# Token choice spread over periods 0 to 8, expert work in periods 9 to 14, and one scatter-add for two experts

## The chip, the cores and the metric

The kernel runs on one NeuronCore of a Trainium2 chip. The metric is the device time of one execution in microseconds (us): before the change the median of three runs is 1363.7 us, with 1360.01 and 1367.55 us as the lowest and the highest. The engines are named as the profile names them: PE (matmuls; PEld is its weight load), DVE (vector), ACT (scalar and activation functions), POOL (GpSimd, which also issues the indirect DMAs) and SP (which issues all other DMAs). Each engine works through its own queue in order. An instruction that waits therefore holds up everything behind it on its engine.

## What is computed

The program computes two layers of a transformer for 32 sequences of 256 tokens, 8192 tokens of width 128, all in fp32. The change touches only the first layer's mixture of experts (MoE):

```python
xn = layernorm(x)
s  = attn0(xn)                                   # two attention + MLP blocks
# MoE: 64 experts of width 96, each token chooses 8, each expert holds at most 64 tokens
probs = softmax(xn @ router_w.T);  w, ids = top_k(probs, 8);  w = w / w.sum()
valid = (place of the token in its expert's queue, in token order) < 64
y[e]  = (silu(xb[e] @ w_gate[e]) * (xb[e] @ w_up[e])) @ w_down[e]
moe   = sum over a token's valid experts of w * y   +   shared expert(xn)
x = x + s * silu(moe)
```

A second layer follows (linear attention and a MoE with one expert of 32 for each token). It starts from the sums of the first layer, and the change leaves it as it is.

## The kernel before

**Periods.** The 8192 tokens are 16 groups of 512. Two groups make a pair `p`, and a pair passes through the two attention blocks `l`, so there are 16 units `(p, l)`. The loop `for k in range(units + 2)` works in periods: period `k` does the softmax attention of unit `k`, and beside it (`beside(k)`) the second norm and the widening matmuls of unit `k-1`, the narrowing matmuls of unit `k-2`, and the norm and the projections of unit `k+1`. These are generators that `run` takes in turn, a step of each at a time. They set the order in which the program is written. The Tile framework then schedules the instructions onto the engines' queues when the program is built, and that order is fixed at run time.

**The token choice** is more generators in the same periods. `enter(g)` loads and norms a group and writes it to a table in device memory (`tab0`). `choose(p)` takes router logits, exponentials and the eight largest of 64 for each token (L400 and L401 on DVE), writes the weights to `tab0` (L411) and makes a key row for each expert (L418). `shared(g)` is the shared expert (L427 to L439). `search(k)` finds, for a quarter of the tokens, each expert's 64 first tokens: eight rounds of MAX8 and MATCH_REPLACE8 over 1024 keys (L446 and L447). After the last quarter `places()` merges the four quarters (L457 to L474) and leaves the row numbers `gidx` and `sidx`. Which pairs are chosen in which period stands in the dictionary `choosing`, and the quarters stand in `searched`; `share(k)` takes the pairs chosen in period `k-1`.

**The experts.** `experts(q)` handles four experts. It loads their weights, gathers 2 x 128 rows from `tab0` with two indirect DMAs on POOL (L485; rows 0 to 63 are an even expert's, 64 to 127 an odd one's), transposes them (L492), and runs gate and up (L499) and down (L511). Four ACT copies (L519) scale the result by each token's weight. Four indirect DMAs with an add (L523), each of 64 rows, put it into two tables, `moe0[0]` for even and `moe0[1]` for odd experts, in turn. A scatter-add waits until the one before it on the same table has landed. There are 16 such calls, two in each of periods 7 to 14.

**What follows.** `route(g)` starts the second layer. Its loads of `moe0` (L184 and L186) wait for the last scatter-add, POOL adds the two tables (L187), and ACT takes the activation (L191). The first `route` steps are written beside periods 15 to 17.

**Buffers** that the change meets: an expert's weights, gathered rows and scaled outputs (`e_wg`, `e_wd`, `e_gx`, `e_y`) have two buffers each, and the PSUM banks of tag `mm` are two. At the period where the choice has ended, its tiles are freed (`cf.close()`) and the first tiles of the second layer are laid out in their place. The flag `early` of `softmax` gives half of the probability scalings (L607) to ACT instead of DVE (L609).

Of the kernel before, what the change touches and what calls it, by code (L numbers as in the profile page):

```python
# [16 lines left out]
F32 = mybir.dt.float32  # L17
I32 = mybir.dt.int32
U32 = mybir.dt.uint32
AF = mybir.ActivationFunctionType  # L20
ALU = mybir.AluOpType
# [4 lines left out]
P = 128  # L26
BATCH, SEQ, D = 32, 256, 128
T = BATCH * SEQ
# [5 lines left out]
E0, K0, C0, F0 = 64, 8, 64, 96  # L34
# [26 lines left out]
def recurrent_kernel(ctx: ExitStack, tc: tile.TileContext, x, consts, small0, wsd, wgu, wd, small1, bias1, wr, out):  # L61
    nc = tc.nc
    vec, act, pool, pe, sp = nc.vector, nc.scalar, nc.gpsimd, nc.tensor, nc.sync
# [6 lines left out]
    dram = ctx.enter_context(tc.tile_pool(name="dram", bufs=1, space=DRAM))  # L70
    psum = ctx.enter_context(tc.tile_pool(name="psum", bufs=4, space=PSUM))

    def bank(tag="mm", bufs=2):
        return psum.tile([P, GW], F32, tag=tag, name=f"ps_{tag}", bufs=bufs)

    tab0 = dram.tile([T + P, D + E0], F32, name="tab0")

    moe0 = [dram.tile([T + P, D], F32, name=f"moe0_{i}") for i in range(2)]
    xslot = dram.tile([S1 * P, D + 1], F32, name="xslot")
    back = dram.tile([T + S1 * P, D], F32, name="back")  # L80
    moe1 = dram.tile([T, D], F32, name="moe1")
# [69 lines left out]
    def room(pool_, gs):  # L151
        for g in gs:
            x_at[g] = pool_.tile([P, GT, D], F32, name=f"x_{g}")
            xt_at[g] = pool_.tile([P, GW], F32, name=f"xt_{g}")
            if g % 4 == 0:
                hots[g // 4] = pool_.tile([P, NT // 4, E1], F32, name=f"hot_{g // 4}")
# [132 lines left out]
    def rolling(steps, lag):  # L289

        live, n = [], 0
        while n < len(steps) or live:
            if n < len(steps):
                live.append(steps[n])
                n += 1
            for _ in range(lag):
                for i in list(live):
                    if next(i, live) is live:
                        live.remove(i)
                    yield  # L300

    def begin(g):
        yield from route(g)
        if g >= INL:
            yield from shared1(g)


    with ExitStack() as c0:


        w0 = c0.enter_context(tc.tile_pool(name="w0", bufs=1, side="right"))
        wk = c0.enter_context(tc.tile_pool(name="wk0", bufs=2, side="right"))
# [130 lines left out]
        def largest(dst, src):  # L443
            for r in range(C0 // 8):
                c8 = dst[:, r * 8 : (r + 1) * 8]
                vec.max(c8, src)  # L446
                found.append(vec.match_replace(out=src, in_to_replace=c8, in_values=src, imm_value=0.0))  # L447
                yield

        gidx = w0.tile([P, E0 // 2], I32, name="gidx")  # L450
        sidx = w0.tile([C0, E0], I32, name="sidx")

        def places():
            top = wf.tile([P, C0], F32, name="top", bufs=1)
            yield from largest(top, cand.rearrange("p q c -> p (q c)"))
            both = wf.tile([E0, 2 * C0], F32, name="both", bufs=1)
            vec.tensor_copy(both[:, :C0], top[:E0])  # L457
            ps = bank()
            pe.matmul(ps[:E0, :C0], ident[:, E0:], top, start=True, stop=True)
            vec.tensor_copy(both[:, C0:], ps[:E0, :C0])  # L460
            first = wf.tile([E0, C0], F32, name="first", bufs=1)
            yield from largest(first, both)

            slot = wf.tile([E0, 2, C0], F32, name="slot", bufs=1)
            vec.scalar_tensor_tensor(slot[:, 0], first, 0.0, ciota, ALU.is_equal, ALU.mult)
            vec.tensor_tensor(slot[:, 0], slot[:, 0], first, ALU.subtract)
            vec.tensor_scalar(slot[:, 0], slot[:, 0], float(T), None, ALU.add)
            vec.tensor_copy(slot[:, 1], slot[:, 0])
            ps = bank()
            pe.transpose(ps[:, :E0], slot.rearrange("e h c -> e (h c)"), ident[:E0, :E0])  # L470
            pairs = ps[:, :E0].rearrange("p (j h) -> p j h", h=2)
            vec.tensor_copy(gidx[:C0], pairs[:C0, :, 0])
            vec.tensor_copy(gidx[C0:], pairs[C0:, :, 1])
            vec.tensor_copy(sidx, ps[:C0, :E0])  # L474
            yield

        def experts(q):

            wg = wk.tile([P, 4, 2 * F0], F32, name="e_wg")
            sp.dma_start(wg, wgu[:, 4 * q : 4 * q + 4])  # L480
            wdn = wk.tile([F0, 4, D], F32, name="e_wd")
            sp.dma_start(wdn, wd[:, 4 * q : 4 * q + 4])
            gx = wk.tile([P, 2, D + E0], F32, name="e_gx")
            for h in range(2):
                pool.indirect_dma_start(  # L485
                    out=gx[:, h], out_offset=None, in_=tab0,
                    in_offset=bass.IndirectOffsetOnAxis(ap=gidx[:, 2 * q + h : 2 * q + h + 1], axis=0),
                )
                yield
            pt = bank("tr", 2)  # L490
            for h in range(2):
                pe.transpose(pt[:, h * P : (h + 1) * P], gx[:, h, :D], ident)  # L492
            xg = wk.tile([P, 4 * C0], F32, name="e_xg")
            act.copy(xg, pt[:, : 4 * C0])
            yield
            gu = bank()
            for u in range(2):
                for e in range(4):
                    pe.matmul(  # L499
                        gu[:F0, (4 * u + e) * C0 : (4 * u + e + 1) * C0], wg[:, e, u * F0 : (u + 1) * F0],  # L500
                        xg[:, e * C0 : (e + 1) * C0], start=True, stop=True,
                    )
            hs = wk.tile([F0, 4 * C0], F32, tag="h", name="e_h")
            act.activation(hs, gu[:F0, : 4 * C0], AF.Tanh, scale=0.5)
            vec.scalar_tensor_tensor(hs, hs, 1.0, gu[:F0, : 4 * C0], ALU.add, ALU.mult)
            vec.tensor_tensor(hs, hs, gu[:F0, 4 * C0 :], ALU.mult)
            yield
            yp = bank()
            for e in range(4):
                at = (e % 2) * C0  # L510
                pe.matmul(  # L511
                    yp[at : at + C0, (e // 2) * D : (e // 2 + 1) * D], hs[:, e * C0 : (e + 1) * C0], wdn[:, e],
                    start=True, stop=True,
                )
            yield
            ye = wk.tile([C0, 4, D], F32, tag="y", name="e_y")
            for e in range(4):
                at, col = (e % 2) * C0, D + 4 * q + e
                act.activation(  # L519
                    ye[:, e], yp[at : at + C0, (e // 2) * D : (e // 2 + 1) * D], AF.Copy,  # L520
                    scale=gx[at : at + C0, e // 2, col : col + 1],
                )
                pool.indirect_dma_start(  # L523
                    out=moe0[e % 2], out_offset=bass.IndirectOffsetOnAxis(ap=sidx[:, 4 * q + e : 4 * q + e + 1], axis=0),
                    in_=ye[:, e], in_offset=None, compute_op=ALU.add,
                )
                yield

# [180 lines left out]
        qkv, wide, mid = {}, {}, {}  # L709
# [25 lines left out]


        entered = {0, 1}
        choosing = {0: (0,), 1: (1, 2), 2: (3,), 3: (4, 5), 4: (6,), 5: (7,)}
        searched = {2: (0,), 3: (1,), 4: (2,), 6: (3,)}

        def front(k):

# [21 lines left out]
        def share(k):  # L764
            for p in choosing.get(k - 1, ()):
                for g in (2 * p, 2 * p + 1):
                    yield from shared(g)

        def some(steps, n):
            for _ in zip(range(n), steps):  # L770
                yield

        begun = rolling([begin(g) for g in range(NG)], 2)
        for k in range(units + 2):
            if k == 7:
                cf.close()
                works.append(ctx.enter_context(tc.tile_pool(name="first_work", bufs=1)))
                begin1(ctx.enter_context(tc.tile_pool(name="first", bufs=1)))
            if k == 16:
                ca.close()  # L780
                works.append(ctx.enter_context(tc.tile_pool(name="mid_work", bufs=2)))
                room(ctx.enter_context(tc.tile_pool(name="mid", bufs=1)), range(EARLY, 9))
            steps = [beside(k), front(k), search(k), share(k)]
            steps += [experts(q) for q in range(E0 // 4) if 7 + q // 2 == k]
            if k < units:
                gs, l = unit(k)
                steps = [softmax(gs, l, qkv, k < 7), *steps]
            more = {15: 10, 16: 20, 17: 12}.get(k)
            if more:
                steps.append(some(begun, more))  # L790
            drain(run(*steps))
# [3 lines left out]
    wk = ctx.enter_context(tc.tile_pool(name="wk1", bufs=2))  # L795
# [37 lines left out]
    ps = bank()  # L833
# [285 lines left out]
```

## Time and profile before

| | |
|---|---|
| median of three runs | 1363.7 us (1360.01 to 1367.55) |
| the profiled execution | 1377.67 us, span 1375.7 us |
| PE, DVE, ACT, POOL busy | 90%, 69%, 57%, 50% of the span |
| granted TensorE clock, mean | 0.963 |
| scatter-adds L523 | 64, 92.5 us on POOL, mean 1445 ns |
| gathers L485 | 32, each 1010 ns in a steady period |
| last scatter-add starts at | 730.5 us |

The profiled execution is 14 us longer than the median of the runs, so differences within it are read rather than its total. Matmuls are pipelined and their ends are modelled, so PE "busy" is not PE at its peak. A period is read off from the first of the 16 softmax exponentials (L600) of its unit: period 1 runs from 64.1 to 121.8 us, period 7 from 403.8 to 451.2, period 14 from 710.0 to 766.6.

### The profile page before, as it was taken

To read this page: it belongs to the slowest core of one execution; us is meant where nothing else is said; L and a number is where in the kernel's file an instruction comes from. 1 tells how busy PE (TensorE), PEld (TensorE's weight loads), DVE (VectorE), ACT (ScalarE), POOL (GpSimd) and SP (SyncE) were. 2 spreads that over 40 slices of the span, in tenths; PEclk is the share of its full clock that TensorE was granted. 3 is DMA by queue.
4 is the path that set the end of the run, shared out by engine and by line. 5 is a ranking of instruction groups with operands and counts; after the bars stand their busy time and mean duration, and the time that the engine had idled before them with its cause. 6 is when DMAs were issued, how large, how long until landed. Compare 5 with 4: busy or idle time off the path is not lost.

```text
span 1375.7 us, 22877 instructions
## 1 busy us (share of the span) xinstructions
PE 1239.4 (90%) x7425; PEld 870.5 (63%) x7425; DVE 944.6 (69%) x3079; ACT 777.5 (57%) x1842; POOL 686.8 (50%) x1052
## 2 busy tenths in 40 slices
PE   6988999899989999999997968799988899999797
PEld 4545665656655776667765655566565678788763
DVE  4679898978965566665665865777756565656437
ACT  1775556576646667676674665443634545545343
POOL 6354428272246766667646463533665343443440
PEclk9999999999989999999998988899999999999999
DMA  6021323310221222122201141413110557666567
GB/s 188 11 54 54 105 84 98 102 45 16 93 72 37 55 49 46 21 50 55 49 9 37 47 125 45 121 36 116 34 41 31 164 180 214 198 194 199 180 197 206
DMA packets 135591, 125.81 MB, mean 91 GB/s; under 512 B 17616, under 2 KB 110768, under 8 KB 135344
## 3 DMA queue, kind: packets, MB, share of 16 engines
q1 hardware_dynamic: 123696, 108.57, 26.4%
q0 software_dynamic: 11776, 15.78, 5.0%
q8 instruction: 59, 0.97, 0.3%
q14 instruction: 60, 0.49, 0.1%
HBM read 83.63 MB, written 40.68 MB: 90 GB/s over the span
## 4 chain that ended last, share of the span: by engine, by line
PE 56%; DVE 16%; POOL 9%; ACT 8%; issue 6%; DMA 4%; SPq 0%; POOLq 0%; another core or an unknown queue 0%; ACTq 0%; DVEq 0%
PE ps_mm L680 7%; PE ps_mm L662 6%; PE ps_sc L585 4%; PE ps_mm L626 3%; PE ps_tr L617 3%; PE ps_tr L131 3%; PE ps_mm L557 3%; PE ps_mm L987 2%; PE ps_sc L887 2%; POOL bn_rs L111 2%; PE ps_mm L567 2%; POOL back L992 2%; PE ps_tr L916 2%; PE ps_sc L978 2%; PE ps_mm L640 2%
## 5 line engine op out<-in xcount | busy, mean ns | idle before, releaser
L992 POOL DMA_INDIRECT back<-e_ys,e_toi x96 | 96.3, 1003 | 134.6 <-ACT e_ys L991 113.6
L600 ACT ACTIVATE a_pr<-ps_sc,a_nm 128x256 f32<-128x256 f32 x256 | 119.2, 478 | 68.2 <-DVE a_nm L591 68.1
L110 POOL TENSOR_SCALAR bn_rs<-bn_mv 128x4 f32<-128x4 f32 x112 | 26.2, 234 | 240.9 <-DVE bn_mv L109 216.2
L662 PE MATMUL ps_mm<-xt,sw 128*128 128x512 f32 x256 | 136.5, 638 | 2.6 <-ACT r_ex L397 2.0
L124 POOL TENSOR_SCALAR z<-s_rows,bn_rs 128x128 f32<-128x128 f32 x256 | 128.6, 514 | 6.9
L680 PE MATMUL ps_mm<-sw,m_h 128*128 128x128 f32 x1024 | 128.7, 280 | 2.9 <-ACT a_at L632 1.1
L680 PEld LDWEIGHTS ps_mm<-sw,m_h 128*128 128x128 f32 x1024 | 120.4, 193 | 14.1 <-issue 4.9
L667 DVE SCALAR_TENSOR_TENSOR m_h<-m_h,m_z 128x512 f32<-128x512 f32 x128 | 88.8, 699 | 48.2 <-ACT m_h L666 47.6
L523 POOL DMA_INDIRECT moe<-e_y,sidx x64 | 92.5, 1445 | 57.8 <-ACT e_y L519 41.2
L111 POOL TENSOR_TENSOR bn_rs<-bn_rs,power 128x4 f32<-128x4 f32 x112 | 113.8, 1016 | 1.3
L664 ACT ACTIVATE m_z<-ps_mm,fold 128x512 f32<-128x512 f32 x128 | 86.9, 687 | 39.1 <-PE ps_mm L662 38.8
L591 DVE TENSOR_REDUCE a_nm<-ps_sc 128x2 f32<-128x512 f32 x128 | 83.1, 680 | 34.9 <-PE ps_sc L585 29.9
L978 PE MATMUL ps_sc<-e_xt,e_w 128*128 128x128 f32 x768 | 100.3, 276 | 3.2 <-ACT e_xt L965 2.2
L978 PEld LDWEIGHTS ps_sc<-e_xt,e_w 128*128 128x128 f32 x768 | 93.1, 192 | 9.6 <-issue 6.4
L585 PE MATMUL ps_sc<-a_qk,a_qk 64*128 64x256 f32 x512 | 96.8, 417 | 0.4 <-ACT a_pr L600 0.3
L617 PEld LDWEIGHTS ps_tr<-con,a_pr 128*128 128x128 f32 x512 | 59.4, 145 | 40.6 <-issue 21.2
L617 PE MATMUL ps_tr<-con,a_pr 128*128 128x128 f32 x512 | 76.3, 283 | 9.4 <-ACT a_pt L618 5.9
L666 ACT ACTIVATE m_h<-m_z 128x512 f32<-128x512 f32 x128 | 80.3, 636 | 1.6
L852 POOL DMA_INDIRECT xslot<-s_rows,dest x64 | 68.3, 1068 | 24.1 <-issue 18.5
L626 PE MATMUL ps_mm<-a_pt,a_v 128*64 128x256 f32 x512 | 73.2, 405 | 5.6 <-ACT e_y L519 2.8
L618 ACT COPY a_pt<-ps_tr 128x512 f32<-128x512 f32 x128 | 70.6, 590 | 9.4 <-PE ps_tr L617 7.9
L987 PE MATMUL ps_mm<-e_w,e_hs 128*128 128x128 f32 x384 | 61.7, 288 | 14.3 <-DVE e_hs L984 10.4
(235 smaller groups left out, 2964.6 us busy)
## 6 DMA issues: line engine op xcount, KB each, us to landing
e_w<-in_wr_dram SPq DMA_DIRECT2D x96, 384.0 KB
xslot<-zero SPq DMA_DIRECT2D x4, 1548.0 KB
e_x<-xslot SPq DMA_DIRECT2D x24, 258.0 KB
e_wg<-in_wgu_dram SPq DMA_DIRECT2D x16, 384.0 KB
x_in<-in_x_dram SPq DMA_DIRECT2D x16, 256.0 KB
tab<-s_rows SPq DMA_DIRECT2D x16, 256.0 KB
moe<-s_y SPq DMA_DIRECT2D x16, 256.0 KB
moe<-zero SPq DMA_DIRECT2D x4, 1024.0 KB
```

The lines of the kernel that those rows point to most:

```text
L111: pool.tensor_tensor(rs[:, 0], rs[:, 0], power, ALU.pow)
L124: ins = pool.tensor_scalar(dst[:, j], src[:, j], rs[:, 1, j : j + 1], rs[:, 0, j : j + 1], ALU.add, ALU.mult)
L523: pool.indirect_dma_start(out=moe0[e % 2], out_offset=bass.IndirectOffsetOnAxis(ap=sidx[:, 4 * q + e : 4 * q + e + 1], axis=0), in_=ye[:, ...
L585: pe.matmul(sc[h][:, j * SEQ : (j + 1) * SEQ], qk[0][hd, q0 : q0 + P], qk[1][hd, b * SEQ : (b + 1) * SEQ], start=True, stop=True,)
L600: act.activation(pr[:, n], sc[h][:, j * SEQ : (j + 1) * SEQ], AF.Exp, bias=nm[:, n : n + 1], accum_out=su[:, n : n + 1],)
L617: pe.transpose(pts[:, n * P : (n + 1) * P], pr[:, n, k * P : (k + 1) * P], ident)
L626: pe.matmul(av[h * DPH : (h + 1) * DPH, :SEQ], v[:, 2 * b + k, h * DPH : (h + 1) * DPH], pt[:, k, h], start=k == 0, stop=k == 1,)
L662: pe.matmul(ps, par("w1", l * FF0 + f * P, P), xt, start=True, stop=True)
L680: pe.matmul(ps[:, j * D : (j + 1) * D], hs[f][:, j * P : (j + 1) * P], par("w2", l * FF0 + f * D, D), start=f == 0, stop=f == 3,)
L978: pe.matmul(ps[:, c * P : (c + 1) * P], wt[:, c * P : (c + 1) * P], xt[:, j * P : (j + 1) * P], start=True, stop=True,)
L987: pe.matmul(yp[:, :D], hs[:, c * P : (c + 1) * P], wt[:, 2 * F1 + c * D : 2 * F1 + (c + 1) * D], start=c == 0, stop=c == 1,)
L992: ins = pool.indirect_dma_start(out=back, out_offset=bass.IndirectOffsetOnAxis(ap=toi[:, j : j + 1], axis=0), in_=ys[:, j], in_offset=None,)
```

## The change

Four edits go together.

1. The two sum tables become the two halves of one table `sums0` of 2 x (8192 + 128) rows, and `sidx` holds, in rows 64 to 127, the odd expert's token numbers plus 8320. One scatter-add now writes 128 rows, an even and an odd expert's together: 32 of them instead of 64. The four scaling copies on ACT remain, two ahead of each scatter-add.
2. One pair is chosen in each of periods 0 to 7 (before: eight pairs in periods 0 to 5, two of them in periods 1 and 3), and the four searches stand in periods 2, 4, 6 and 8 (before: 2, 3, 4 and 6).
3. The 16 expert calls start in period 9 and are dealt out as 3, 3, 3, 3, 2, 2 (before: two in each of periods 7 to 14). In a period of three, the first and the third run one after the other in one chain, and the second runs beside them.
4. The choice's tiles are freed at period 9 instead of 7, and `early` holds until then.

```diff
-    moe0 = [dram.tile([T + P, D], F32, name=f"moe0_{i}") for i in range(2)]
+    sums0 = dram.tile([2 * (T + P), D], F32, name="sums0")
+    moe0 = [sums0[i * (T + P) : (i + 1) * (T + P)] for i in range(2)]
...
-        sidx = w0.tile([C0, E0], I32, name="sidx")
+        sidx = w0.tile([P, E0 // 2], I32, name="sidx")
...
-            vec.tensor_copy(sidx, ps[:C0, :E0])
+            vec.tensor_copy(sidx[:C0], pairs[:C0, :, 0])
+            vec.tensor_scalar(sidx[C0:], pairs[C0:, :, 1], float(T + P), None, ALU.add)
...
-            ye = wk.tile([C0, 4, D], F32, tag="y", name="e_y")
-            for e in range(4):
-                at, col = (e % 2) * C0, D + 4 * q + e
-                act.activation(
-                    ye[:, e], yp[at : at + C0, (e // 2) * D : (e // 2 + 1) * D], AF.Copy,
-                    scale=gx[at : at + C0, e // 2, col : col + 1],
-                )
+            ye = wk.tile([P, 2, D], F32, tag="y", name="e_y")
+            for h in range(2):
+                for u in range(2):
+                    at = slice(u * C0, (u + 1) * C0)
+                    col = D + 4 * q + 2 * h + u
+                    act.activation(ye[at, h], yp[at, h * D : (h + 1) * D], AF.Copy, scale=gx[at, h, col : col + 1])
                 pool.indirect_dma_start(
-                    out=moe0[e % 2], out_offset=bass.IndirectOffsetOnAxis(ap=sidx[:, 4 * q + e : 4 * q + e + 1], axis=0),
-                    in_=ye[:, e], in_offset=None, compute_op=ALU.add,
+                    out=sums0, out_offset=bass.IndirectOffsetOnAxis(ap=sidx[:, 2 * q + h : 2 * q + h + 1], axis=0),
+                    in_=ye[:, h], in_offset=None, compute_op=ALU.add,
                 )
...
-        choosing = {0: (0,), 1: (1, 2), 2: (3,), 3: (4, 5), 4: (6,), 5: (7,)}
-        searched = {2: (0,), 3: (1,), 4: (2,), 6: (3,)}
+        choosing = {0: (0,), 1: (1,), 2: (2,), 3: (3,), 4: (4,), 5: (5,), 6: (6,), 7: (7,)}
+        searched = {2: (0,), 4: (1,), 6: (2,), 8: (3,)}
...
+        def chain(*steps):
+            for i in steps:
+                yield from i
+
+        FIRST, working = 9, (3, 3, 3, 3, 2, 2)
...
-            if k == 7:
+            if k == 9:
...
-            steps += [experts(q) for q in range(E0 // 4) if 7 + q // 2 == k]
+
+            qs = range(sum(working[: max(0, k - FIRST)]), sum(working[: max(0, k - FIRST + 1)]))
+            steps += [chain(*(experts(q) for q in qs[i::2])) for i in range(2)]
...
-                steps = [softmax(gs, l, qkv, k < 7), *steps]
+                steps = [softmax(gs, l, qkv, k < 9), *steps]
```

## The prediction

> **What bounds the kernel now.** I read the page's slices first (PE at 8 to 9 tenths nearly everywhere), then busy time by period, then the groups of one steady period, the waits at the two seams, and the chain of work. Busy time by period (stretch, length, then busy us and count of PE, PEld, DVE, ACT, POOL, the granted clock, DMA share, GB/s); the first row is period 1, the last period 14:
>
> ```profile
> 64.10:121.80 57.70, 50.62 (x246) 29.58 (x246) 48.92 (x192) 36.91 (x99) 31.31 (x63) 0.88 0.18 46
> 121.80:180.00 58.20, 53.06 (x307) 34.48 (x306) 51.16 (x151) 36.29 (x93) 23.63 (x48) 1.00 0.27 87
> 180.00:239.00 59.00, 53.13 (x314) 35.62 (x313) 54.33 (x194) 37.53 (x98) 33.01 (x64) 0.97 0.33 99
> 239.00:298.30 59.30, 53.28 (x307) 34.33 (x306) 52.10 (x163) 36.22 (x92) 28.69 (x59) 1.00 0.25 81
> 298.30:349.40 51.10, 47.88 (x285) 31.12 (x283) 41.16 (x108) 34.71 (x90) 13.96 (x29) 1.00 0.06 16
> 349.40:403.80 54.40, 48.21 (x261) 31.52 (x262) 44.66 (x155) 30.79 (x78) 23.76 (x46) 0.91 0.29 93
> 403.80:451.20 47.40, 44.37 (x292) 30.80 (x289) 27.51 (x82) 30.34 (x80) 26.69 (x35) 0.96 0.19 40
> 494.30:537.50 43.20, 42.87 (x287) 29.77 (x285) 27.87 (x81) 29.86 (x79) 28.79 (x41) 1.00 0.21 44
> 710.00:766.60 56.60, 48.14 (x289) 32.43 (x287) 33.54 (x102) 32.58 (x85) 29.93 (x42) 0.91 0.16 33
> ```
>
> Periods 8 to 13 take 43.1 to 43.2 us each, and PE idles 0.3 us in them: PE is the bound there, and nothing that leaves POOL or DVE helps. Periods 1 to 4 run PE and DVE both at about nine tenths and take 58 to 59 us. The change moves work between these two kinds of period. From 64.1 to 710.0 us it is 645.9 us, all that the change reorders but the end of period 14.
>
> One steady period by group (count, busy us, mean ns):
>
> ```profile
> L523 POOL DMA_INDIRECT moe<-e_y,sidx x8 | 11.5, 1437 | 5.3 <-ACT e_y L519 3.5 <-issue 1.8
> L485 POOL DMA_INDIRECT e_gx<-tab,gidx x4 | 4.0, 1010 | 1.2 <-issue 0.6 <-DMA moe<-e_y,sidx 0.3 <-ACT a_at L632 0.3
> L499 PE MATMUL ps_mm<-e_xg,e_wg 128*96 128x64 f32 x32 | 3.3, 247 | 0.0
> L511 PE MATMUL ps_mm<-e_wd,e_h 96*64 96x128 f32 x16 | 1.3, 285 | 0.0
> L492 PE MATMUL ps_tr<-con,e_gx 128*128 128x128 f32 x4 | 0.8, 286 | 0.0
> ```
>
> The scatter-adds are the largest POOL group, but POOL is busy 28.8 of 43.2 us. Two expert calls cost PE 3.3+1.3+0.8 = 5.4 us by rows; the rows of the period sum to 47.6 against 42.87 busy (neighbours overlap), a factor 0.90, so one call is 2.4 us of PE. The seam in period 6 shows as PE's waits, the other in the chain of work (start, us, what):
>
> ```profile
> PE ps_mm L470 <- DVE bn_mv L109: 3.3, 1, 3.3
> PE ps_tr L492 <- DMA e_gx<-tab,gidx: 2.0, 1, 2.0
> ```
>
> ```profile
> 730.53 3.34 DMA moe<-e_y,sidx
> 733.88 2.66 DMA c_m<-moe
> 736.68 1.27 POOL c_g L187
> ```
>
> The last scatter-add lands 3.34 us after its issue; it holds the loads of the next layer, through POOL's sum holds ACT, and PE then waits 5.9 us for ACT at 739.
>
> **The Trainium skill.** "Perfetto Trace Analysis", Optimization Strategy, says that a kernel whose most-contended engine changes over time may gain from interleaving its regimes. Here the regimes are already interleaved with attention; the trace shows no slack on PE where the experts go, so that advice only shifts idle time. "Perfetto Trace Analysis", DMA Instruction — SWDGE, says an indirect DMA's interval ends with descriptor generation and hides the movement; the trace agrees (1.40 us on POOL, 3.34 to landing). "DMA: Bandwidth & Descriptors", Anatomy of one DMA, says generation is small and the fixed cost is mostly the write receipt; I find 3.34-1.40 = 1.94 us after POOL is free. "TensorE: Matmul & The Clock Gate", What's actually happening, says an idle window of about 3.4 us halves PE's clock; the mean clocks 0.88 and 0.91 stand in just the periods with gaps.
>
> **The change, part by part.** PE's work is unchanged: the same matmuls. So the sum is one of idle time and of where it falls.
>
> *Choice spread.* By rows with the same 0.90, a pair costs PE about 9.8 us (router, key transposes, shared expert, entry) and DVE 6.8 us for choosing (MAX8 1.5, MATCH_REPLACE8 1.6 and its loads 0.6, reductions and small steps 3.1), 2.7 for the shared expert, 3.3 for entry; a search is 20 us of DVE (16 x 1.21 plus loads). In the built order of the changed kernel, period 7 has the same DVE mix as period 5 before (17 norm steps, 10 search, 26 choice, 4 shared), and period 8 that of period 6. Period 7 is therefore 51.1 us and period 8 54.4. Periods 2 to 6 each have one choice and one shared pair, like period 5, 6 to 9 search steps instead of 10, but 32 or 64 norm steps instead of 17. PE's work is period 5's, 48 us; DVE's is about 40 in periods 3 and 5 and 46 to 50 in 2, 4 and 6. I take 51.1 for the first two and 53.5 for the other three, since before, periods with DVE near PE kept PE gaps of 4 to 7 us. Sum of 2 to 7: 3 x 51.1 + 3 x 53.5 = 313.8. Period 1 loses one choice (6.8 us of DVE) and 15 norm steps, gains two search steps: DVE 48.9 to about 42. At the old ratio 48.9/57.7 that is 49; some of its clock loss (0.12 x 57.7 = 6.9 us of half clock) should go, so 47.5. The ACT scalings that `early` adds in periods 7 and 8 (16 x 0.5 us) lie under 16 us of ACT idle; without that cover they would cost 8 us and save DVE 6.
>
> *Experts.* Period 9 takes the seam: old period 7's 47.4, plus one call 2.4, plus 1.4 because in the built order PE now waits for the second gather too (1.01 and 0.3 between issues), plus 0.5 as in the next line: 51.7. Periods 10 to 12: 43.1 + 2.4 + 0.5 = 46.0 each, 138.0; the 0.5 is my estimate for the third call's own chain (transposed copy 0.38, tanh 0.41, two DVE steps 0.41 each, under only about 1.7 us of other matmuls). Period 13 stays 43.1.
>
> *Scatter-adds.* POOL work falls, but every scatter-add now waits for the previous one to land, and the norms (L110 to L124) stand behind it on POOL. No row shows 128 rows with an add. Below it is 1.40 us (64 rows), above twice 1.44 = 2.87. The plain 128-row scatter takes 1.00, at most 7.8 ns a row, so 64 rows more are up to 0.5: I take d = 1.9, and 2.3 from there to landing (1.94 and 0.4 more for twice the packets, 0.57 us for 64 rows). In a period of three calls, POOL does S1, three gathers, S2, a gather, S3, S4, S5, two gathers, half a norm, S6, the rest. From S1 to S5: (d+4.2) + 3(d+2.3) = 18.7 us. The third call's output is ready 18.8 us after S1's start (matmuls between, by their row means), so S5 is on time. After the third call's down matmul POOL needs 7.65+2d = 11.5 us to the finished norm (copies 0.9, two scatter-adds and gaps 2d+0.6, gathers 2.6, norm 3.55); PE has 14.8 us of other matmuls before it transposes it. Slack 3.3 us, so cost 0; it is gone at d = 2.5. The buffer of scaled outputs is free about 3 us before the third call wants it. At the end, four chained scatter-adds land 4 x 4.2 = 16.8 us after the first; before, eight landed at 733.88, 16.7 us after 717.19. I take -1 for it, at d = 1.44 it is -3.
>
> *SP* sees the same loads; the third call's weights come two calls ahead, into a buffer freed long before.
>
> Sum: 47.5 + 313.8 + 54.4 + 51.7 + 138.0 + 43.1 = 648.5, against 645.9: +2.6, with the end -1: +1.6. In the profiled execution that is 1377.67 to 1379.3; on the median of the runs, 14 us lower, 1363.7 to about 1366. Half a per cent, 6.8 us, is about what a measurement of this kernel can tell from no change.
>
> **Rivals.** *DVE stays the bound in the mixed periods* (slower): periods 2 to 7 average 54.5 instead of 52.3, +13 us, 1379. For it: periods 2 to 4 before kept 58 to 59 us at DVE 51 to 54, so time followed DVE. Against it: period 5, at 41. It decides when DVE needs more than about 47 us in such a period. *The scatter chain* (slower): at d = 2.87, six d of each three-call period exceed the cover by 6 x 2.87 - 14.85 = 2.4 us, four times, +9.6: 1376; it starts at d = 2.5. *PE alone bounds the mixed periods* (faster): with DVE eased they run at PE's 48 plus 1.7, 49.7 x 6 = 298, -16, and period 1 at 45: 1348 to 1351. For it: PE idles only 0.3 us once DVE is light. Against it: period 5, with DVE at 41 of 51, still idled 3.2. *The change does not do what it says*: excluded, since the built order has the experts in periods 9 to 14 and 32 scatter-adds.
>
> **How the numbers follow.** Forecast, within 6.8 us of before: 0.38 (own range 1358 to 1371). DVE rival 0.22, scatter rival 0.15: slower 0.37. PE rival: faster 0.25. Leaving a tenth on each side, the range is 1352 (deep in the PE rival) to 1384 (the slow rivals partly together).
>
> **What would show it.** Periods 2 to 7 at 51 to 53.5 us; period 8 at 54; periods 10 to 12 at 46 with PE idle under 1 us; L523's successor at 1.9 us; no wait of PE for a norm on POOL. Wrong would be: PE waiting for `z` from POOL in periods 9 to 12, DVE above 92% in periods 2 to 6, or a half clock in the three-call periods.

## The result and the profile after

The change makes the kernel slightly faster: 1350.48 us (median of 12 runs, 1347.23 to 1357.38) against 1361.65 us before (12 runs), ratio 0.9914, 95% interval 0.9893 to 0.9934. Forecast was no change, 1366 us, with a range from 1352 us. The measured time lies 1.5 us below that range.

The profiled execution after has a span of 1347.1 us. Before it was 1375.7, but that difference must not be read off whole. From the start of period 15 to the end PE, DVE, ACT and POOL each run the same instructions in the same order in both kernels, and the two profiles show 609.1 us before and 593.0 after. A later profile of the kernel after, on another chip, shows 609.5 in that stretch and repeats what lies ahead of it within 2 us a period (experiment 1), and the medians of this kernel on the two chips, 1350.5 and 1367.1 us, differ by as much. The first profile before, 1377.67 us, lies above all twelve timed runs of its kernel. So those 16 us come from the chip or the execution and not from the change. What the change does lies ahead of period 15: from the start of period 1 to that of period 15 it is 702.5 us before and 689.4 after, 13.1 less, which agrees with the ratio (0.0086 x 1361.65 = 11.7).

Busy time by period of the kernel after (stretch, length, then busy us and count of PE, PEld, DVE, ACT, POOL, granted clock, DMA share, GB/s): periods 1 to 4, then 8, 9, 10, 13 and 14.

```profile
64.70:112.70 48.00, 42.97 (x228) 24.97 (x227) 43.75 (x145) 33.71 (x89) 26.63 (x53) 0.96 0.15 39
112.70:161.20 48.50, 48.36 (x277) 31.32 (x277) 41.88 (x149) 33.43 (x87) 25.36 (x49) 1.00 0.25 83
161.20:214.60 53.40, 48.80 (x283) 31.97 (x282) 39.78 (x119) 34.88 (x89) 18.56 (x37) 0.97 0.13 35
214.60:264.70 50.10, 47.63 (x284) 31.73 (x283) 44.45 (x155) 33.55 (x88) 26.40 (x54) 1.00 0.29 90
...
417.30:470.80 53.50, 45.62 (x266) 29.87 (x265) 45.01 (x157) 30.85 (x78) 22.79 (x44) 0.97 0.29 95
470.80:518.20 47.40, 45.89 (x311) 31.88 (x310) 28.32 (x83) 33.16 (x85) 28.67 (x40) 1.00 0.27 59
518.20:564.60 46.40, 45.37 (x313) 31.80 (x311) 28.89 (x84) 32.41 (x84) 29.73 (x41) 1.00 0.28 61
...
657.40:700.30 42.90, 42.48 (x287) 29.72 (x285) 25.77 (x65) 30.08 (x79) 20.73 (x27) 1.00 0.21 44
700.30:754.10 53.80, 44.91 (x289) 30.61 (x287) 33.24 (x101) 32.70 (x84) 25.31 (x38) 0.94 0.15 33
```

The periods that carry the choice now take 48 to 53 us, where four of them took 58 to 59. The three-call periods take 46.4 with PE idle for 1 us. The clock column matters too: the half-clock stretches in periods 1 to 13 add up to 30.7 us before and 10.2 us after. PE's busy time in these periods falls from 607.4 to 601.6 us for the same 3707 matmuls, and its idle time from 38.5 to 34.0. So of the 10.4 us gained up to period 14, 5.8 are shorter busy time and about 4.5 are shorter gaps. PE is busy for 28.3 us inside half-clock stretches before and for 10.3 us after. At half speed these 18 us cost up to 9, an estimate, so the clock is large enough to explain the 5.8 us. It is not all of it: a period of two calls, at full clock throughout, also falls from 42.8 to 42.5 us of busy PE.

PE's waits around the seam of periods 8 and 9 (what waits, for what: us in all, times, longest):

```profile
PE ps_tr L494 <- DMA e_gx<-tab,gidx: 3.7, 1, 3.7
PE ps_mm L471 <- DVE bn_mv L110: 3.3, 1, 3.3
```

Both waits of the old seam are still there, now inside period 8. The third one of before, 2.8 us in period 7 for ACT's copies of `e_y`, is gone.

The two groups that carry the indirect DMAs in period 10 (line, operation, count, busy us and mean ns, idle before and its releaser), and the chain at the end of period 14 (start, us, what):

```profile
L524 POOL DMA_INDIRECT sums<-e_y,sidx x6 | 9.6, 1599 | 12.5 <-ACT e_y L523 5.0 <-DMA sums<-e_y,sidx 3.9 <-ACT a_pt L619 3.1
L487 POOL DMA_INDIRECT e_gx<-tab,gidx x6 | 5.9, 982 | 1.8 <-issue 0.9 <-PE ps_mm L627 0.3 <-ACT a_pr L601 0.3
```

```profile
719.43 3.23 DMA sums<-e_y,sidx
...
723.11 2.97 DMA c_m<-sums
...
726.22 1.27 POOL c_g L188
```

A 128-row scatter-add takes 1.60 us on POOL where a 64-row one took 1.44. The chain of scatter-adds shows as POOL idle time (3.9 us in the period), and no wait of PE for POOL is listed there.

### The profile page after: what moved, and what is told of

Same layout as the page of the kernel before. It is cut to its first block, busy times and chain, and to the rows that moved or that the text cites. A ratio compares the mean times of both kernels' runs of the same rounds, so it can differ in the third digit from the quotient of the medians.

```text
span 1347.1 us, 22826 instructions
## 1 busy us (share of the span) xinstructions
PE 1226.4 (91%) x7425; PEld 864.0 (64%) x7425; DVE 940.0 (70%) x3064; ACT 785.7 (58%) x1858; POOL 650.4 (48%) x1020
## 5 line engine op out<-in xcount | busy, mean ns | idle before, releaser
L601 ACT ACTIVATE a_pr<-ps_sc,a_nm 128x256 f32<-128x256 f32 x256 | 119.1, 478 | 59.2 <-DVE a_nm L592 59.1
L663 PE MATMUL ps_mm<-xt,sw 128*128 128x512 f32 x256 | 134.1, 630 | 1.6 <-ACT e_y L523 0.9
L112 POOL TENSOR_TENSOR bn_rs<-bn_rs,power 128x4 f32<-128x4 f32 x112 | 116.7, 1043 | 1.3
L665 ACT ACTIVATE m_z<-ps_mm,fold 128x512 f32<-128x512 f32 x128 | 87.3, 685 | 28.3 <-PE ps_mm L663 27.9
L524 POOL DMA_INDIRECT sums<-e_y,sidx x32 | 51.1, 1598 | 80.5 <-ACT e_y L523 39.5
L619 ACT COPY a_pt<-ps_tr 128x512 f32<-128x512 f32 x128 | 71.7, 590 | 12.8 <-PE ps_tr L618 11.7
L558 PE MATMUL ps_mm<-xt,sw 128*128 128x512 f32 x128 | 69.0, 645 | 6.5 <-ACT xt L546 2.7
```

The source lines that it names most:

```text
L112: pool.tensor_tensor(rs[:, 0], rs[:, 0], power, ALU.pow)
L601: act.activation(pr[:, n], sc[h][:, j * SEQ : (j + 1) * SEQ], AF.Exp, bias=nm[:, n : n + 1], accum_out=su[:, n : n + 1],)
L663: pe.matmul(ps, par("w1", l * FF0 + f * P, P), xt, start=True, stop=True)
L665: act.activation(z, ps, AF.Identity, bias=fold[:, l, 3 + f : 4 + f])
```

## Experiments

In all these runs the kernel before takes 1378 to 1380 us on the chip at hand. Each is compared with runs of the kernel before on the same chip, and the lengths of periods are read from its profile. "P1 to P13" below is the stretch from the start of period 1 to that of period 14: 646.0 us before, 635.6 after.

### 1. Both kernels once more

The unchanged kernel before, and later the unchanged kernel after.

> The kernel before, unchanged: a second profiled execution of it. Reading A (the extra 16 us that the first profile of the kernel before has behind period 14 is that execution's own): the stretch from the start of period 15 to the end takes about 593 us as in the profile after, and the starts of periods 1 to 15 repeat within 1 us. Reading B (the change shortens the part behind period 14): it takes about 609 us again. Half clock: if the dips in period 1 (two of 6.8 us), in periods 6 and 7 (6.8, 3.4 and 3.4 us) belong to the schedule, they are there again; if they are chance, they move.

> The kernel after, unchanged, beside the three others on one chip: its periods repeat within 0.5 us (47.9, 48.6, 53.4, 50.0, 51.3, 50.3, 51.1, 53.5, 47.4, 3 x 46.4, 42.8, 53.8), its ratio to before is about 0.991. If the part behind period 15 takes 609 to 616 us here as in the other runs of this kind, the 593 us of the first profile of the kernel after belong to that chip and not to the change.

The kernel before repeats: P1 to P13 646.1 us, half clock again twice 6.8 us in period 1 (at 87.0 and 104.1) and 3.4 and 10.2 us at 390.8 and 397.7. So these dips belong to the schedule. One of 3.4 us in period 0 is new, and the length at a place can change (in period 8 of the kernel after 3.4 us, and 6.8 in its repeat). Its part behind period 15 is again long (609.6 us), which by itself looked like reading B. The kernel after settles it: ratio 0.9922 (0.9893 to 0.9951), P1 to P13 634.7 us, periods 1 to 7 and 10 to 13 within 0.2 us of the first profile, period 8 1.8 us shorter (PE waits 1.2 us for the gather there instead of 3.7) and period 9 0.7 longer. Its last part, on the first chip and on this one:

```profile
754.10:1347.10 593.00, 528.49 (x3182) 399.17 (x3179) 390.62 (x1323) 297.05 (x593) 271.31 (x362) 0.95 0.45 134
```

```profile
753.80:1363.30 609.50, 531.89 (x3182) 401.69 (x3179) 393.39 (x1323) 297.26 (x593) 269.93 (x362) 0.95 0.44 131
```

No shortening behind period 15 can be put down to the change. Why the profiles differ there was not looked into. The other runs below, with the same order of instructions in that part, take 601.5 to 615.7 us for it.

### 2. The scatter-add alone

The kernel after with the old places of choice and experts (the choice's tiles freed at period 7 and `early` ended there, as before):

```diff
-        choosing = {0: (0,), 1: (1,), 2: (2,), 3: (3,), 4: (4,), 5: (5,), 6: (6,), 7: (7,)}
-        searched = {2: (0,), 4: (1,), 6: (2,), 8: (3,)}
+        choosing = {0: (0,), 1: (1, 2), 2: (3,), 3: (4, 5), 4: (6,), 5: (7,)}
+        searched = {2: (0,), 3: (1,), 4: (2,), 6: (3,)}
...
-            steps += [chain(*(experts(q) for q in qs[i::2])) for i in range(2)]
+            steps += [experts(q) for q in range(E0 // 4) if 7 + q // 2 == k]
```

> Only the first edit: one table and 128-row scatter-adds, with the old choice and two expert calls in each of periods 7 to 14. Theory 1 (the gain is in where the choice lies): 0 to -3 us against before, periods 8 to 13 unchanged at 43.1, the last scatter-add landing 1 to 3 us earlier against the start of period 14. Theory 2 (the shorter POOL work of the scatter-adds is a main part): -5 us or more. If the chain of waits hurt, slower.

Ratio 0.9949 (0.9930 to 0.9968), -7 us. That is the number of theory 2, but POOL's time is not the main cause: in the steady periods POOL is busy 24.4 us instead of 28.8, and they give only 0.3 each. P1 to P13 is 639.8 us, 6.3 less than in the kernel before on this chip. Most of it, 4.5 us, is in periods 6 and 7. First these two before on this chip, then periods 6 to 8 of this run:

```profile
350.30:405.90 55.60, 48.41 (x261) 31.48 (x262) 44.77 (x155) 30.92 (x78) 24.43 (x47) 0.90 0.28 91
405.90:452.10 46.20, 43.20 (x292) 30.19 (x289) 27.36 (x81) 30.35 (x79) 25.71 (x33) 0.98 0.20 41
```

```profile
350.40:403.60 53.20, 46.67 (x266) 30.53 (x265) 45.18 (x157) 30.92 (x79) 22.60 (x43) 0.94 0.29 95
403.60:447.70 44.10, 42.90 (x285) 29.74 (x284) 27.62 (x81) 30.50 (x79) 22.71 (x34) 1.00 0.19 43
447.70:490.60 42.90, 42.46 (x287) 29.69 (x285) 27.58 (x82) 30.20 (x78) 24.41 (x37) 1.00 0.19 44
```

One cause stands in ACT's order. In the kernel before the eight scaling copies of the first two calls are written as four single steps each, and the last two fall behind four exponentials. PE's next matmul waits for them (first PE's wait, then ACT's copies and the first of the four exponentials by start, us, instruction; from the first profile):

```profile
PE ps_mm L626 <- ACT e_y L519: 2.8, 1, 2.8
```

```profile
413.30 1.00 ACT L519 ACTIVATE e_y<-ps_mm,e_gx 64x128 f32<-64x128 f32 x3
...
414.93 0.36 ACT L519 ACTIVATE e_y<-ps_mm,e_gx 64x128 f32<-64x128 f32 x1
415.19 0.46 ACT L600 ACTIVATE a_pr<-ps_sc,a_nm 128x256 f32<-128x256 f32 x1
...
417.12 0.62 ACT L519 ACTIVATE e_y<-ps_mm,e_gx 64x128 f32<-64x128 f32 x2
```

With the 128-row form two copies go out in each step, and the same eight stand together. In this run:

```profile
411.66 1.50 ACT L523 ACTIVATE e_y<-ps_mm,e_gx 64x128 f32<-64x128 f32 x4 [0.85 <-PE ps_mm L513]
...
413.79 1.49 ACT L523 ACTIVATE e_y<-ps_mm,e_gx 64x128 f32<-64x128 f32 x4
```

The wait of 2.8 us is gone. The half clock in these two periods also falls, from 13.7 us in both profiles before to 6.8. In the first of them 3.4 us of it followed this wait. In its repeat none did, and 10.2 us followed PE's wait for the first gather (3.0 us; 2.4 in this run). So the wait for the copies is read from the traces, and how the rest of the 4.5 us divides stays open. No run changed the order of the copies alone.

### 3. The schedule alone

The kernel before with edits 2 to 4, and so with 64-row scatter-adds into two tables.

```diff
-        choosing = {0: (0,), 1: (1, 2), 2: (3,), 3: (4, 5), 4: (6,), 5: (7,)}
-        searched = {2: (0,), 3: (1,), 4: (2,), 6: (3,)}
+        choosing = {0: (0,), 1: (1,), 2: (2,), 3: (3,), 4: (4,), 5: (5,), 6: (6,), 7: (7,)}
+        searched = {2: (0,), 4: (1,), 6: (2,), 8: (3,)}
...
-            steps += [experts(q) for q in range(E0 // 4) if 7 + q // 2 == k]
+            steps += [chain(*(experts(q) for q in qs[i::2])) for i in range(2)]
```

> Only edits 2 to 4: choice spread, experts in periods 9 to 14, with the old 64-row scatter-adds into two tables. Theory 1: -8 to -12 us against before, periods 2 to 7 at 50 to 51 us as in the kernel after; the three-call periods within 1 us of 46.4. Theory 2: half of the gain or less, the three-call periods over 47.5 because eight 64-row scatter-adds become twelve (POOL then has about 36 of 46 us).

Ratio 1.0221 (1.0192 to 1.0250): slower by 30 us, which neither theory had. Periods 1 to 8 are those of the kernel after within 0.1 us. The loss is in the three-call periods, 60.5, 55.4, 55.1 and 54.9 us against 47.4 and 46.4. Period 10, and PE's longest wait in it (`z` is the normed rows that POOL writes):

```profile
532.20:587.60 55.40, 48.62 (x313) 32.94 (x311) 28.34 (x83) 32.60 (x84) 36.37 (x47) 0.94 0.24 51
```

```profile
PE ps_tr L131 <- POOL z L124: 5.5, 1, 5.5
```

PE waits for a norm that stands on POOL behind the scatter-adds, and half clock follows (6.8 us). In the kernel after, the third call's down matmuls end at 542.2 us, the norm is finished on POOL at 554.8 and PE transposes it at 556.8. In this run the down matmuls end at 557.4, the norm is finished 14.7 us later, at 572.1, and PE has reached it at 565.4. So the old scatter-adds cost in two ways: POOL needs 2.1 us more, and PE arrives after 8.0 us of other work instead of 14.6, because the built order puts the norm's transposes earlier: 37 matmuls stand between the third call's down matmuls and these transposes, where the kernel after has 65. Period 9 loses more than the others, 13.1 us, and was not followed up.

### 4. Packed experts with the old choice

The kernel after with the old `choosing` and `searched`; the choice's tiles are freed at period 7 and `early` ends there as before.

```diff
-        choosing = {0: (0,), 1: (1,), 2: (2,), 3: (3,), 4: (4,), 5: (5,), 6: (6,), 7: (7,)}
-        searched = {2: (0,), 4: (1,), 6: (2,), 8: (3,)}
+        choosing = {0: (0,), 1: (1, 2), 2: (3,), 3: (4, 5), 4: (6,), 5: (7,)}
+        searched = {2: (0,), 3: (1,), 4: (2,), 6: (3,)}
...
-                steps = [softmax(gs, l, qkv, k < 9), *steps]
+                steps = [softmax(gs, l, qkv, k < 7), *steps]
```

> The scatter-add edit and the experts packed in periods 9 to 14, but the old choice (pairs in periods 0 to 5, searches in 2, 3, 4 and 6). Theory 1 (the spread of the choice makes the gain): periods 1 to 5 as before (57.7, 58.2, 59, 59, 51), about 38.5 us in periods 7 and 8 without expert work, 46.4 in 9 to 12, so PE's work only moves: 0 to -5 us against before. Rival (packing the experts makes it): -9 us or more. If periods 7 and 8 without experts can't run at PE's pace, they stay above 40 and the kernel is slower than before.

Ratio 0.9995 (0.9973 to 1.0017): no gain without the spread. Periods 7 and 8 without experts, then a three-call period:

```profile
400.30:440.00 39.70, 38.54 (x233) 26.00 (x232) 25.40 (x77) 25.84 (x66) 16.54 (x33) 1.00 0.01 3
440.00:479.80 39.80, 39.07 (x237) 26.45 (x235) 25.49 (x78) 26.26 (x68) 13.97 (x29) 1.00 0.00 1
...
526.40:573.10 46.70, 45.39 (x313) 31.79 (x311) 28.72 (x84) 32.55 (x84) 29.98 (x41) 1.00 0.27 60
```

A period takes 39.7 us with no call, 42.9 with two (experiment 2) and 46.7 with three. The first two calls cost 1.6 us each and the third 3.8. Packing therefore is not free. Together with experiment 2, P1 to P13 goes 646.1 (before), 639.8 (scatter-add: -6.3), 643.7 (packing: +3.9), 635.6 (spread of the choice, with edit 4: -8.1). The last step is the largest gain, and the scatter-add edit is what makes packing bearable. How much of the last step is `early` is not clear. With the spread, but `early` ending at period 7 (experiment 7), P1 to P13 is 645.0, as if the spread alone gave nothing; by the ratios (0.9954, against 0.9995 here and 0.9922 for the kernel after) `early` is under half of it.

### 5. More work for DVE in the mixed periods

The kernel after with idle DVE instructions in the softmax of periods 3 to 7 (four softmax steps in a period; 3 or 6 instructions in each; `now[0]` is the period).

```diff
                         vec.tensor_scalar(pr[:, n], pr[:, n], su[:, n : n + 1], None, ALU.mult)
+                if now[0] in range(3, 8):
+                    for _ in range(3):
+                        vec.tensor_scalar(spare0, pr[:, 3], 0.5, None, ALU.mult)
```

> The kernel after with 12 idle DVE instructions of 128x256 (about 0.34 us each, 4.1 us) added to the softmax of each of periods 3 to 7. DVE busy becomes about 44 in periods 3, 5 and 7 and 48.6 in 4 and 6. Theory D of the prediction (a period's time follows DVE, its busy time plus 5.6): periods 4 and 6 go from 50 to 54, periods 3, 5 and 7 stay, +8 us in all. Theory P (PE bounds these periods and DVE has slack up to about 48): every one of the five periods within 1 us of before, 0 to +3 us in all.

> As the run with 12, with 24 such instructions (8.2 us a period): DVE about 48 in periods 3, 5 and 7 and 52.7 in 4 and 6. Theory D: 53.7 in 3, 5 and 7, 58.3 in 4 and 6, +23 us in all. Theory P: about 51 to 52 in 3, 5, 7 and 55 in 4 and 6 (DVE's own time and 2.5 us), +10 to +12.

Ratios 0.9998 (0.9981 to 1.0016) and 1.0083 (1.0057 to 1.0108); against the 0.9922 of experiment 1 that is +10 and +22 us. Periods 4, 5 and 8 with 12 instructions, and then with 24:

```profile
212.90:266.90 54.00, 49.90 (x281) 33.29 (x281) 47.04 (x165) 33.57 (x87) 21.81 (x42) 0.94 0.24 79
266.90:317.50 50.60, 48.35 (x289) 31.37 (x287) 43.53 (x131) 35.13 (x91) 25.73 (x51) 1.00 0.15 43
...
422.60:481.70 59.10, 49.09 (x264) 31.09 (x264) 45.61 (x159) 31.18 (x78) 24.04 (x47) 0.94 0.26 86
```

```profile
214.90:270.30 55.40, 49.96 (x284) 32.47 (x283) 50.37 (x179) 34.16 (x88) 25.72 (x50) 0.97 0.25 82
270.30:321.70 51.40, 48.43 (x286) 31.42 (x285) 44.28 (x142) 34.83 (x90) 22.16 (x44) 1.00 0.14 37
...
430.00:493.70 63.70, 52.25 (x266) 32.05 (x265) 47.41 (x160) 31.73 (x78) 25.64 (x50) 0.87 0.24 79
```

The even periods follow DVE: its 44.5, 47.0 and 50.4 us in period 4 give 50.1, 54.0 and 55.4, its busy time plus 5 to 7. Theory P, which had 48.6 us of DVE for nothing, falls with the 12. But the time does not grow by a fixed amount for each us of DVE. Theory D had 58.3 for the 24, because it added 8.2 us where DVE's busy time grew by 5.9, and theory P's 55 is nearer to that run (55.4, and 56.8 in period 6). With the 12, PE's longest wait in period 4 is one for DVE that takes 0.6 us in the kernel after, and 6.8 us of half clock set in during it:

```profile
PE ps_mm L390 <- DVE s_rows L694: 2.8, 1, 2.8
```

Periods 5 and 7 stay at 50.6 to 51.5, near PE's own 48 us. Period 3 takes 51.0 and 53.5 us, and 53.4 in the kernel after. All three have this wait:

```profile
PE ps_mm L437 <- DVE s_h L433: 2.2, 1, 2.2
```

It is followed by 3.4 us of half clock in the kernel after and with 24, and by none with 12. The difference of 2.4 us goes with the half clock, and more DVE work is not its cause. What neither theory had is period 8, which gets no added instruction and grows from 53.5 to 59.1 and 63.7. The built order moves one and then two of the 1.2-us search steps of the last quarter out of period 7 into it, and PE's wait for the places grows from 3.3 to 4.9 us.

### 6. More work for POOL

The kernel after with three POOL instructions behind each scatter-add, which read the scaled outputs.

```diff
                     in_=ye[:, h], in_offset=None, compute_op=ALU.add,
                 )
+                for _ in range(3):
+                    pool.tensor_scalar(spin, ye[:, h], 0.5, 0.0, ALU.mult, ALU.add)
                 yield
```

> The kernel after with three POOL instructions of 128x128 (about 0.52 us each, which read the scaled outputs) added at each 128-row scatter-add: POOL time for one pair of experts rises from 1.6 to 3.16 us, about what two 64-row scatter-adds took (2 x 1.43 and a gap). Theory 1 (what makes packing slow with the old scatter-adds is POOL's time ahead of the norm): the three-call periods go from 46.4 to 50 or more with PE waiting for z from POOL, as in the run with the old scatter-adds (55), +15 to +35 us in all. Rival (it is the old order of four scatter-adds and their copies, or their waits for each other): the three-call periods stay within 1.5 us of 46.4, +0 to +6 us in all, as my formula for the chain gives (from S1 to S5 18.3 us against 18.8).

Ratio 1.0009 (0.9994 to 1.0024), about +12 us against the kernel after. Periods 9 to 12 take 50.9, 48.4, 48.5 and 50.1. Period 10:

```profile
521.60:570.00 48.40, 46.04 (x313) 31.82 (x311) 28.79 (x84) 32.59 (x85) 36.18 (x61) 1.00 0.26 58
```

It lies between the two: +2 us (periods 10, 11) to +3.7 us a period, not 9. POOL is as busy as in experiment 3 (36.2 against 36.4 us), but PE waits only 1.1 us for `z`:

```profile
PE ps_tr L132 <- POOL z L125: 1.1, 2, 0.6
```

The transposes still stand 65 matmuls, about 15 us, behind the third call's down matmuls. The norm is even finished later than in experiment 3, 16.6 us after them instead of 14.7. So a late norm alone does not make that loss: a smaller part is POOL's time, and the rest goes with the earlier place of the transposes in PE's order and the half clock that follows. No run changed that place alone.

### 7. `early` until period 7 only

The kernel after with all probability scalings of periods 7 and 8 on DVE.

```diff
-                steps = [softmax(gs, l, qkv, k < 9), *steps]
+                steps = [softmax(gs, l, qkv, k < 7), *steps]
```

> The kernel after with one edit taken back: half of the probability scalings stay on ACT in periods 0 to 6 only, so that periods 7 and 8 give eight more scalings each (8 x 0.34 = 2.7 us) to DVE and 8 x 0.5 us less to ACT. If a period is the longer of PE's time with about 3 us of gaps and DVE's time plus 6 (theory D, as the two runs with added DVE work showed): period 7 stays within 1 us of 51.1 (DVE 40.7 to 43.4), period 8 grows by 2.7 to 5 (DVE is its bound), +3 to +5 us in all. If ACT were short there: faster.

Ratio 0.9954 (0.9938 to 0.9970), +4 us by the ratios and +9 in the profile. Periods 7 and 8:

```profile
367.30:417.00 49.70, 48.07 (x284) 31.24 (x283) 40.68 (x113) 31.14 (x81) 15.38 (x30) 1.00 0.08 22
417.00:480.40 63.40, 52.42 (x265) 31.87 (x264) 49.05 (x168) 29.31 (x71) 26.21 (x51) 0.89 0.25 80
```

Again two search steps move from period 7 into period 8, whose DVE work rises by 4.0 us, and the time by 9.9, twice what was expected. Period 7 is 1.4 us shorter.

### 8. Three tries on the seam of period 8

First the merging of the search results moved to the start of period 9, with calls dealt out as 2, 3, 3, 3, 3, 2 and the choice's tiles freed one period later:

```diff
-                if q == NG // 4 - 1:
-                    yield from places()
...
-            steps += [chain(*(experts(q) for q in qs[i::2])) for i in range(2)]
+            calls = [chain(*(experts(q) for q in qs[i::2])) for i in range(2)]
+            steps += [chain(places(), run(*calls))] if k == FIRST else calls
```

> The kernel after, with the merging of the four search results (16 more rounds on DVE, two small matmuls) moved from the end of period 8 to the start of period 9, ahead of the experts, which are dealt out as 2, 3, 3, 3, 3, 2; the choice's tiles are freed one period later. In the kernel after, PE waits 3.3 us for the merged places and 3.7 us for the first gather, both inside period 8 (53.5 us, PE idle 8). Theory 1 (these waits and the half clock behind them cost what they show): period 8 falls to about 46 to 47, period 9 loses a call but waits for its first gather with other work in front, -4 to -7 us against the kernel after, ratio to before about 0.987. Rival (the seam only moves into period 9, where PE has nothing else to do first): within 2 us of the kernel after, 0.991.

Then the search of period 8 with two of its steps to one of the others, and with it all probability scalings of that period on ACT:

```diff
-            steps = [beside(k), front(k), search(k), share(k)]
+            steps = [beside(k), front(k), double(search(k)) if k == 8 else search(k), share(k)]
...
-                    if early and n % 2 == 0:
+                    if (early and n % 2 == 0) or early == 2:
```

> The kernel after with the search of period 8 taking two steps for each step of the others, so that the places stand in the middle of the period on DVE and PE instead of at its end, and the first gathers ahead of the period's last matmuls. If the 7 us of waits at the seam (places 3.3, gather 3.7) go as far as DVE's own 45.5 + 6 allows: period 8 from 53.5 to about 51, -2 to -4 us in all against the kernel after. If the search only pushes the norms and activations on DVE back and PE waits for those: 53 to 57, 0 to +4.

> As the run with the doubled search, and all probability scalings of period 8 on ACT (8 x 0.34 = 2.7 us less on DVE, 8 x 0.5 us more on ACT, which idles 22.7 us there). By theory D period 8 falls by another 2 to 3 us, to 48 to 49: -5 to -7 us in all against the kernel after, ratio to before about 0.987. If the seam's waits are not DVE's: no further gain.

None beats the kernel after. Moving the merge gives ratio 0.9956 (0.9939 to 0.9974): period 8 falls to 44.1 us, more than hoped, but period 9 takes 59.9:

```profile
418.80:462.90 44.10, 43.06 (x260) 28.70 (x260) 39.65 (x122) 30.63 (x79) 18.58 (x38) 1.00 0.20 73
462.90:522.80 59.90, 51.69 (x290) 35.63 (x288) 32.49 (x116) 30.62 (x79) 28.97 (x45) 0.89 0.23 61
```

PE waits 5.2 us for gathers there and runs 13.7 us at half clock. The seam moves. The doubled search gives 0.9915 (0.9884 to 0.9946) and with the scalings 0.9919 (0.9889 to 0.9949), beside 0.9922 for the kernel after. Period 8 is 55.6 and 54.8 us: the gather wait is gone, but the wait for the places stays (1.5 and 3.7 us), and PE also waits for the scalings (2.4 and 1.1 us). Period 9 takes 46.1 and 46.0, and nothing is gained in all.

## Why the prediction was wrong

The forecast by period against the profile after:

| period | forecast | measured | difference |
|---|---|---|---|
| 1 | 47.5 | 48.0 | +0.5 |
| 2, 4, 6 | 53.5 each | 48.5, 50.1, 50.3 | -11.6 |
| 3, 5, 7 | 51.1 each | 53.4, 51.2, 51.1 | +2.4 |
| 8 | 54.4 | 53.5 | -0.9 |
| 9 | 51.7 | 47.4 | -4.3 |
| 10 to 12 | 138.0 | 139.2 | +1.2 |
| 13 | 43.1 | 42.9 | -0.2 |
| sum | 648.5 | 635.6 | -12.9 |
| period 14 (an end of -1 on 56.6) | 55.6 | 53.8 | -1.8 |

**The step that failed first: "46 to 50 in 2, 4 and 6".** This is DVE's work in the even periods. The forecast took it to be near PE's 48 us and put 5.5 us of PE gaps on top, 53.5 in all, since periods with DVE near PE had kept gaps of 4 to 7. DVE measured 41.9, 44.5 and 44.5 us, and PE's gaps were 0.1, 2.5 and 2.8. The rule behind the step holds: when experiment 5 puts DVE in period 4 at 47.0 and 50.4, PE's gaps are 4.1 and 5.4. What was mis-sized is DVE's load. The norm steps were added at their full row means, 47 of them at about 0.215 us, which with the smaller number of search steps gives the forecast's 46 to 50. Period 4 of the kernel after has these rows (x count, busy us, mean ns):

```profile
L109 DVE BATCH_NORM_STATS2 bn_st<-s_rows 128x6 f32<-128x128 f32 x24 | 5.9, 265 | 0.0
...
L110 DVE BATCH_NORM_AGGREGATE bn_mv<-bn_st 128x2 f32<-128x6 f32 x32 | 5.1, 166 | 0.0
...
L109 DVE BATCH_NORM_STATS2 bn_st<-x_in 128x6 f32<-128x128 f32 x8 | 2.0, 261 | 0.0
```

That is 13 us by rows. But all DVE instructions of this period add up to 54.9 us by their durations, and DVE is busy for 44.5. In period 5 before, with fewer norm steps, they add up to 47.1 and it is busy for 41.2. So 7.8 us more by rows are 3.3 us of engine time: short instructions overlap in the records. Periods 4 and 5 of the kernel after, with 64 and 32 norm steps and with nine and seven search steps, are 4.8 us of busy DVE apart. Less the two search steps of 1.21 us, 32 norm steps cost about 2.4 us, or 0.07 each, an estimate from these rows. The factor 0.90 used for PE and for one pair was not used here, and it would have taken only 1 us off these 10.

**The second: "period 9 takes the seam: old period 7's 47.4".** The 4.3 us of old period 7 were taken for part of the moved seam. But most of them go with the change's first edit alone (experiment 2: 44.1 us, against 47.4 and 46.2 in the two profiles before), which removes PE's wait of 2.8 us for the old scatter-add's single copies. The seam proper, the waits for places and gather, did move (3.3 and 3.7 us against 3.3 and 2.0), but stands in period 8, which was forecast as 54.4 with only the old seam in it and came out at 53.5. The 1.4 us added for the second gather were right in kind and in the wrong period.

**Right.** Period 1 (47.5 against 48.0), and the 51.1 of periods 5 and 7. Period 3 is 2.3 longer, because 3.4 us of half clock follow PE's wait for the shared expert there (experiment 5). Three-call periods at 46.0 (46.4), though for a reason only half seen: a third call costs 3.5 to 3.8 us, not 2.9, while the two-call period became 0.2 to 0.3 shorter. That `early` costs nothing in periods 7 and 8: without it the kernel is slower (experiment 7). What it would cost without idle time on ACT no run shows. Period 14 gained 2.8 us where 1 was forecast: the last scatter-add lands 22.4 us after its start instead of 23.9, and its half clock falls from 10.2 to 6.8 us.

**The scatter chain.** The forecast took d = 1.9 us and 4.2 us to landing; 1.60 and 3.4 were measured, and the slack ahead of the norm was about 2 us instead of 3.3. The rival was right that such a chain can cost time: experiment 6, with 2.94 us for a scatter-add and its three added instructions (1.68 + 3 x 0.42), costs 2 to 3.7 us a period, where the formula, fed with the shorter landing, gave nothing. Whether it starts near d = 2.5 no run shows. Nothing in the forecast saw that the same schedule with two 64-row scatter-adds loses 30 us, where the rival had 9.6 at d = 2.87, since the place of the norm's transposes in PE's order changes with it.

**The rivals.** "PE alone bounds the mixed periods" named the measured time, 1348 to 1351, with a chance of 0.25. Its reason holds for the odd periods only. Periods 2 to 7 average 50.8 us, between its 49.7 and the forecast's 52.3, and the even ones still follow DVE (experiment 5). It was 6.4 us too short for periods 2 to 7 and 3 for period 1, and periods 9 and 14, where it kept the forecast's values, came out 6.1 shorter. That its sum came so near is in part luck. "DVE stays the bound" at 54.5 us was the forecast's own DVE error made larger.

**A term that was hardly there: the clock.** The forecast counted "idle time and where it falls", with half clock in period 1 alone. Over half of the gain up to period 14 (5.8 of 10.4 us) is shorter busy time of PE, most of it by size the clock: period 1 keeps 3.4 us of half clock of 13.7, and the seam in period 8 has 3.4 where periods 6 and 7 had 13.7. The forecast also read period 1 wrongly: 0.12 x 57.7 = 6.9 us is the clock lost in 13.7 us of half clock, not its length. And half clock did not stand "in just the periods with gaps": PE idled 5 and 6 us in periods 2 and 4 before at full clock.

## What to carry to other kernels

Split a change into its edits before pricing it: here the scatter-add was worth 6 us under the old schedule and decided between -12 and +30 us under the new one, so the parts do not add. When short instructions are added, size an engine's load from the busy time of a comparable stretch (overlaps counted once), not from row means times counts. When a wait is carried over to a new place, ask first which edit it came from.

## What the runs showed of the hardware

- Twice the rows in one scatter-add cost 0.16 us more on POOL (1.44 to 1.60 us) and hardly anything to landing (the last one 3.34 us before and 3.23 after; 3.4 is the median of the 32).
- Half clock followed PE gaps shorter than one of its 3.4-us stretches: a gap of 2.7 us at 86.0 us (3.4 us from 90.5) and of 2.2 us at 162.1 (3.4 us from 165.5) after; in the kernel before 6.8 us from 86.2 after a single gap over 0.4 us in the 10 us before it, of 1.2 us. It did not always follow: in period 3 the same gap of 2.2 us brought 3.4 us of half clock in the kernel after and none in the run with 12 added DVE instructions (53.4 and 51.0 us). The Trainium skill, "TensorE: Matmul & The Clock Gate", What's actually happening, speaks of at least one idle window of about 3.4 us; here the measurement decides.
- The order of the instructions on PE, DVE, ACT and POOL is the same in two executions of a kernel on two chips. Up to period 14 the lengths of the periods away from the seams agree within 0.5 us, those beside a seam (6 and 7 before, 8 and 9 after) within 2 us, while the part behind it took 593.0 and 609.5 us for the kernel after.
